# Two cross-attention query projections by Strassen's method in a fused decoder kernel

## The chip, the core and the metric

The kernel runs as one program on one core of a Trainium2 chip. The core has a matrix engine (TensorE, PE in the profile; its weight loads are PEld), VectorE (DVE), ScalarE (ACT), GpSimd (POOL) and SyncE (SP), which issues the DMAs. Each takes its own instructions in order, and they wait for each other by semaphores. The metric is the device time of one execution in microseconds: 1154.2 us is the median of three runs of the kernel before (1152.12 to 1158.6).

## What is computed

A decoder layer and a gated cross-attention layer, all in float32, over 16 sequences of 128 tokens and 512 features, with 16 heads of 32:

```python
ln_out = layernorm(hidden_states, ln1_s, ln1_b)
q, k, v = jnp.split(ln_out @ w_qkv + b_qkv, 3, axis=-1)
x = hidden_states + merge_heads(attention(q, k, v, ltor_mask)) @ w_ao + b_ao
ln_out = layernorm(x, ln2_s, ln2_b)
q = ln_out @ w_q + b_q                       # the product that is changed
k, v = jnp.split(encoder_states @ w_kv + b_kv, 2, axis=-1)
x = x + merge_heads(attention(q, k, v, cross_mask)) @ w_co + b_co
ln_out = layernorm(x, ln3_s, ln3_b)
x = x + gelu(ln_out @ w1 + b1) @ w2 + b2
# then: a gated cross-attention of x with the layer-normalized context, and its residual
```

The heads are split before each attention. Scores are scaled, masked, and turned into probabilities by a softmax.

## The kernel before

The 16 sequences are worked in four groups of four; a group's activations are 512 x 512 (512 features by 4 x 128 tokens), kept with features on the partitions in four chunks of 128. The decoder's attention is eight sections, one after the other: self-attention A0 to A3 (one a group), then cross-attention B0 to B3. An MLP and four gated sections D0 to D3 follow. A section is 16 steps, one for each unit of four heads (number 0 to 3) of a sequence.

`attend` (line 689) writes the order of all engines out by hand; nothing reorders it. In step k of a section TensorE does the scores of a new sequence (every fourth step), the mixing with the values of an earlier one (beside the scores) and its output projection `mo` (two steps after), and the products of the next section's `jobs`. VectorE turns a normalized unit (a 32 x 32 transpose; it is then sent to DRAM and fetched back as `pT`), takes reciprocals of the exponentials' sums, takes the least value of the unit masked in the step before, and scales new scores out of PSUM. ACT does the exponentials. POOL multiplies a unit by the reciprocals (`s<-s,sum`, called a normalization here), and adds the mask to a new unit (`s<-s,mask`). So POOL's mask of step k-1 releases VectorE's least values in step k, these release ACT's exponentials, and VectorE's reciprocal in step k+1 releases POOL's normalization there. `afterwards` (line 80) puts an operation off to the beginning of the next step, where `due` (line 83) issues what was put off, VectorE's first.

Beside section i, `jobs` computes query, key and value of section i+1, and `prepare(p)`, called in step p, prepares section i+2: layer normalization with statistics on VectorE, a power (`rstd`) and a row addition (`x<-x,bco_row`) on POOL, the way through DRAM that turns it (`back`), and in steps 12 to 15 the scaling into `lnT` by ACT. In steps 11 and 13 the first three sequences of x[g] are copied to DRAM, because their place in SBUF serves as scratch; `tokens_again` fetches them back in steps 5, 9 and 13 of the group's own section.

Key and value are computed by Strassen's method in Winograd's form (`block_product`, line 409): operands are cut into quarters of 256 x 256, sums of quarters are formed (`left_blocks` for a weight, `right_blocks` for activations, four additions each), and seven products of quarters, each four float32 matmuls of 128x256, are added up. Blocks 1, 6 and 7 share the PSUM bank mm0 and are copied out by ACT in the step that issues them; blocks 5 and 3 share the bank mm1; blocks 2 and 4 take one of two banks "pt" in turn with mixing and output projection. Blocks 2, 3, 4 and 5 are added into the result by VectorE, one step after. `CROSS_BLOCKS` (line 507) says which block is issued in which step: the key's in steps 4 to 11, the value's in steps 10 to 15. The query is computed directly, in four chunks of four matmuls of 128x512 (`project_chunk`, line 338) in steps 0, 1, 3 and 5, with the banks mm0 and mm1 in turn, and one copy by ACT each, put off by a step. The float32 matmuls stand twice in the profile's counts.

The key's and value's four token sums (`right_blocks(encT, tokens_at)`) are formed by POOL in steps 0 to 3, in scratch in x[g] and one in place. The weight sums of key and value are formed once, beside section A3: the key's by VectorE, the value's by POOL.

Of the kernel before, what the change touches and what calls it, by code (L numbers as in the profile page):

```python
# [54 lines left out]
def decoder_then_gated_cross_attention(ctx: ExitStack, tc: tile.TileContext, a: dict, out: bass.AP):  # L55
# [260 lines left out]
    def group_back(t, back, scale=None, bias=None, chunks=range(KC)):  # L316
        for k in chunks:
            chunk_back(t[:, k], back, k, scale, bias)
# [10 lines left out]
    def turn_squares(t, c):  # L329

        nc.vector.transpose(t[:, c], t[:, c])
# [32 lines left out]
    def halves(t):  # L364

        return [[t[:, 2 * i : 2 * i + 2, j * HF : (j + 1) * HF] for j in range(2)] for i in range(2)]
# [4 lines left out]
    def left_blocks(wt, t):  # L371


        (a11, a21), (a12, a22) = halves(wt)
        s3, s2, s4, s1 = (*t, a21)[:4]
        return [a11, a12, s4, a22, s1, s2, s3], [
            (s3, a11, a21, ALU.subtract), (s1, a21, a22, ALU.add), (s2, s1, a11, ALU.subtract),
            (s4, a12, s2, ALU.subtract),
        ]

    def right_blocks(actT, t):

        (b11, b12), (b21, b22) = halves(actT)
        t1, t2, t4 = t
        return [b11, b21, b22, t4, t1, t2, b12], [
            (t1, b12, b11, ALU.subtract), (t2, b22, t1, ALU.subtract), (b12, b22, b12, ALU.subtract),
            (t4, t2, b21, ALU.subtract),
        ]
# [20 lines left out]
    def block_product(out, left, right, turned, name, bias=None):  # L409

        product = quarter_matmuls(left, right, turned, name)
        (c11, c12), (c21, c22) = out

        def copy(dst, mm, half):

            if bias is None:
                nc.scalar.copy(dst, mm)
            else:  # L420
                for o in range(2):
                    nc.scalar.activation(dst[:, o], mm[:, o], AF.Identity, bias=col(bias[0], bias[1] + 2 * half + o))

        def add(dst, one, other, op=ALU.add):
            afterwards("dve", lambda: nc.vector.tensor_tensor(dst, one, other, op))

        mm5 = []

        def last_quarter():
            if len(mm5) == 2:  # L430
                add(c22, mm5[0], c21)

        def job(n):
            if n in (1, 6, 7):
                mm = product(n, "mm0", n == 1)
                copy({1: c11, 6: c12, 7: c21}[n], mm, int(n == 7))
                if n == 7:
                    mm5.append(None)
                    last_quarter()
            elif n == 5:  # L440
                mm5.insert(0, product(n, "mm1", True))
                last_quarter()
            elif n == 2:
                add(c11, product(n, "pt", True), c11)
            elif n == 4:
                add(c21, c21, product(n, "pt", True), ALU.subtract)
            elif n == 3:
                add(c12, product(n, "mm1", False), c12)

        return {n: lambda n=n: job(n) for n in range(1, 8)}  # L450
# [39 lines left out]
    def by_quarters(t):  # L490

        return [[t[:, 2 * j : 2 * j + 2, i * HF : (i + 1) * HF] for j in range(2)] for i in range(2)]
# [15 lines left out]
        {4: (1,), 7: (2, 6), 8: (5,), 9: (7, 4), 11: (3,)},  # L508
        {10: (1,), 11: (2,), 12: (6,), 13: (5, 7), 15: (4, 3)},
    )  # L510
    FIRST_CROSS_BLOCKS = {6: (1,), 7: (2, 6), 8: (5,), 9: (7, 4), 11: (3,)}, CROSS_BLOCKS[1]
    GATED_BLOCKS = (
# [10 lines left out]
    def blocks_plan(products, blocks):  # L523
        out = {}
        for jobs, steps_ in zip(products, blocks):
            for step, ns in steps_.items():
                out.setdefault(step, []).extend(jobs[n] for n in ns)
        return [(jobs, [step] * len(jobs)) for step, jobs in out.items()]
# [148 lines left out]
    def plan(*timed):  # L677

        out = {}
        for jobs, at_ in timed:  # L680
            for job, step in zip(jobs, at_, strict=True):
                out.setdefault(step, []).append(job)
        return out
# [321 lines left out]
    class CrossAttention(Section):  # L1005
# [6 lines left out]
        def prepare(self, p):  # L1012
            g, n = self.g, self.name
            if p == 0:
                if g == 0:
                    w["bco"] = load_row(a["L0_xattn_b_co"], "bco_row")
                self.ln, self.away = ln_tile(n), away_tile(n)
                self.encT = act_tile(f"e{g}", "enc")
            if p < 2 * GB:
                load_turned(self.encT, encoder_rows(g), p // 2, (2 * (p % 2), 2 * (p % 2) + 1))  # L1020
                q = p // 2
                if p % 2 == 0:
                    normalize_and_send(
                        x[g][:, q, :], self.ln[:, q], self.away, n, q, lambda: add_row(g, w["bco"], q)
                    )
            elif p == 9:
                self.back = receive(n, self.away)
                self.lnT = act_tile(n)
            elif p >= 12:
                group_back(self.lnT, self.back, "ln2_s", "ln2_b", [p - 12])  # L1030
            if p in (11, 13):

                for b in ((0, 1), (2,))[p == 13]:
                    keep_part(f"x_{n}", x[g], b)
            if p >= 2 * GB and p % 2 == 0:
                turn_squares(self.encT, p // 2 - GB)
            if g == 0 and p >= 3 * GB:
                load_cross("cq", p - 3 * GB)

        def jobs(self):  # L1040
            g, n, lnT, encT = self.g, self.name, self.lnT, self.encT
            mask = work.tile([P, 2, GB, S], F32, tag="mask", name=f"mask_{g}", bufs=2)
            self.ms, self.ma = mask[:, 0], mask[:, 1]
            nc.sync.dma_start(
                out=self.ms, in_=a["mask_Bx1xSxS2_ff1"][g * GB : (g + 1) * GB, 0].rearrange("b q k -> q b k")
            )
            qkv_tiles(self)
            tokens_at = [x[g][:, b].rearrange("p (o t) -> p o t", t=HF) for b in range(3)]
            token_sides, sums = right_blocks(encT, tokens_at)
            if g == 0:  # L1050
                self.begin()
            products = [
                block_product(halves(self.k), self.k_sides, token_sides, False, f"k_{n}", ("b_k", 0)),
                block_product(by_quarters(self.v), self.v_sides, token_sides, True, f"v_{n}"),
            ]
            return plan(
                ([lambda c=c: self.query_chunk(c) for c in range(KC)], [0, 1, 3, 5]),
                *blocks_plan(products, CROSS_BLOCKS if g else FIRST_CROSS_BLOCKS), ([lambda: mask_terms(self.ms, self.ma)], [7]),
                ([lambda o=o: nc.gpsimd.tensor_tensor(*o) for o in sums], [0, 1, 2, 3]),
                *(self.weights_begin() if g == 0 else decoder[NG + g - 1].tokens_again([5, 9, 13])),  # L1060
            )

# [1 line left out]
            project_chunk(self.q, w["cq"], self.lnT, c, f"q_{self.name}", "b_q", 0, ("mm0", "mm1")[c % 2])  # L1064

        v_bias = "b_cv", 0

        def tokens_again(self, at_, order=range(3)):
            return [([lambda b=b: fetch_part(f"x_{self.name}", x[self.g], b) for b in order], at_)]
# [391 lines left out]
    class FirstGated:  # L1461


        def prepare(self, p):
            if p == 0:
                self.raw = work.tile([P, GB, H], F32, tag="enc", name="enc_D0", bufs=2)
                self.ln, self.away = ln_tile("D0"), away_tile("D0")
            if p in (0, 1):
                for b in (2 * p, 2 * p + 1):
                    nc.sync.dma_start(out=self.raw[:, b, :], in_=a["ctx_2048"][b])  # L1470
            elif p >= 2 * GB:
                key, k = ("gk", "gv")[p // GB - 2], p % GB
                if k == 0:
                    w[key] = wpool.tile([P, KC, H], F32, tag="w", name=f"w_{key}")
                nc.sync.dma_start(out=w[key][:, k], in_=gated[key][:, k])
            if 2 <= p < 6:
                q = p - 2
                normalize_and_send(self.raw[:, q, :], self.ln[:, q], self.away, "D0", q)
            if p >= 12:
                if p == 12:  # L1480
                    next(in_mlp)
                ml.pieces.popleft()()
            if p in (9, 11):
                if p == 9:
                    self.back, self.part = receiver("a0", self.away)
                for m in range(2):
                    self.part(m + 2 * (p == 11))
            if p >= 12:
                if p == 12:
                    self.aT = act_tile("a0", "enc")  # L1490
                group_back(self.aT, self.back, "gamma", "beta", [p - 12])
# [339 lines left out]
```

## Time and profile before

| | before |
|---|---|
| median of three runs | 1154.2 us (1152.12 to 1158.6) |
| the profiled execution | 1150.03 us, its span 1148.3 us |
| granted TensorE clock in it | 1.0 |
| busy: PE, DVE, POOL, ACT | 1127.4, 743.3, 695.4, 611.3 us |
| section B0 (first scores to next section's) | 282.38 to 343.26 us |
| section B1 | 343.26 to 404.15 us |
| section B2 | 404.15 to 465.73 us |

A line of the order of time gives start and duration in us, engine, operation, what is written and read, shapes and count; group numbers are left out of names, so `mm_q_B` is the query of any cross-attention group. Where an engine was idle before, it says for how long and what ended that. Durations include the filling and emptying of an engine; back to back, instructions start closer together than their durations, and the distance of starts is what one costs. All instructions have the line of a helper, L51. `T_B` is lnT, `T_e` the encoder's activations, `s_B` a unit of scores, `sc_B` scores in PSUM. Spans on POOL are rough.

### The profile page before, as it was taken

How to read it: one execution, taken by the hardware profiler on the slowest of the kernel's cores; microseconds unless marked ns; L12 is line 12 of the kernel's file. 1: busy time of each engine (PE TensorE's matmuls, PEld its weight loads, DVE VectorE, ACT ScalarE, POOL GpSimd, SP SyncE). 2: the span in 40 equal slices, each digit the busy share in tenths (PEclk: the TensorE clock that was granted, in tenths of full speed). 3: DMA queues.
4: the chain of work that ended last, by engine and by line, in shares of the span. 5: the costliest groups of instructions: out<-in, count | busy, mean ns of one | idle time of the engine just before them, and what ended most of it. 6: DMA issues, size and time to landing. Idle time of an engine off the chain costs nothing. (4 is left out here: it accounts for less than half of the span.)

```text
span 1148.3 us, 22191 instructions
## 1 busy us (share of the span) xinstructions
PE 1127.4 (98%) x7246; PEld 870.1 (76%) x7246; DVE 743.3 (65%) x1919; ACT 611.3 (53%) x2142; POOL 695.4 (61%) x633
## 2 busy tenths in 40 slices
PE   8999999999999999999999999999999999999998
PEld 7877777667575757546788888888888877878885
DVE  6678988888877776987664634443342237767764
ACT  3467676767676776774231333233222337777663
POOL 6798888788868685773333414443343168545874
PEclk9999999999999999999999999999999999999999
DMA  6588878999888879999786596697446827988975
GB/s 222 153 216 233 221 217 221 260 231 264 211 229 217 229 213 255 294 284 296 243 259 232 183 285 188 198 280 266 156 147 220 268 70 191 246 245 233 266 223 182
DMA packets 325284, 259.81 MB, mean 226 GB/s; under 512 B 83560, under 2 KB 280624, under 8 KB 320304
## 3 DMA queue, kind: packets, MB, share of 16 engines
q1 hardware_dynamic: 325128, 258.38, 78.4%
q8 instruction: 58, 0.95, 0.4%
q14 instruction: 58, 0.48, 0.1%
q10 hardware_dynamic: 40, 0.01, 0.0%
HBM read 163.94 MB, written 94.37 MB: 225 GB/s over the span
## 5 line engine op out<-in xcount | busy, mean ns | idle before, releaser
L51 DVE TENSOR_TENSOR h<-h,h 128x512 f32<-128x512 f32 x80 | 54.8, 686 | 114.4 <-PE h L51 114.3
L51 ACT ACTIVATE h<-h 128x512 f32<-128x512 f32 x64 | 40.3, 630 | 160.9 <-DVE h L51 160.9
L51 ACT ACTIVATE s_A<-s_A,mn_A 128x128 f32<-128x128 f32 x256 | 99.4, 391 | 46.8 <-issue 24.1
L51 ACT ACTIVATE s_B<-s_B,mn_B 128x128 f32<-128x128 f32 x256 | 99.4, 392 | 31.1 <-issue 18.2
L51 POOL TENSOR_TENSOR s_D<-s_D,sum_D 128x512 f32<-128x512 f32 x64 | 66.8, 1043 | 56.1 <-DVE sum_D L51 53.7
L51 ACT ACTIVATE s_D<-s_D,mn_D 128x128 f32<-128x128 f32 x256 | 99.1, 392 | 0.4 <-issue 0.4
L51 POOL TENSOR_TENSOR s_B<-s_B,sum_B 128x512 f32<-128x512 f32 x64 | 67.2, 1051 | 51.5 <-DVE sum_B L51 33.5
L51 POOL TENSOR_TENSOR s_A<-s_A,sum_A 128x512 f32<-128x512 f32 x64 | 66.9, 1046 | 30.4 <-DVE sum_A L51 24.5
L51 POOL TENSOR_TENSOR s_A<-s_A,ma 128x512 f32<-128x512 f32 x64 | 82.3, 1286 | 5.1 <-DVE s_A L51 4.1
L51 POOL TENSOR_TENSOR s_B<-s_B,mask 128x512 f32<-128x512 f32 x60 | 76.8, 1280 | 2.2 <-DVE s_B L51 1.3
L51 POOL TENSOR_TENSOR rstd_aD<-rstd_aD,mhalf 128x1 f32<-128x1 f32 x12 | 6.6, 550 | 115.0 <-DVE rstd_aD L51 101.5
L51 POOL TENSOR_TENSOR sh<-h 128x512 f32<-128x512 f32 x32 | 40.8, 1274 | 50.5 <-ACT h L51 49.6
L51 PE MATMUL h<-T_C,w 128*128 128x256 f32 x256 | 61.2, 382 | 2.2 <-DVE h L51 2.2
L51 PE MATMUL h<-T_C,t 128*128 128x256 f32 x256 | 60.6, 379 | 1.0 <-DVE h L51 1.0
L51 PE MATMUL h<-sx,t 128*128 128x256 f32 x256 | 60.7, 380 | 0.5 <-POOL sx L51 0.5
L51 PE MATMUL o<-t,sh 128*128 128x256 f32 x256 | 60.5, 379 | 0.0
L51 PE MATMUL o<-w,h 128*128 128x256 f32 x256 | 60.5, 379 | 0.0
L51 PE MATMUL o<-t,h 128*128 128x256 f32 x256 | 60.5, 379 | 0.0
L51 DVE CUSTOM_DVE_ANT_0 s_D<-sc_D,gmask 128x128 f32<-128x128 f32 x256 | 57.2, 283 | 1.3 <-DMA turned_x<-x_D 0.7
L51 PE MATMUL mo_B<-w_co,mT_B 128*128 128x512 f32 x128 | 57.5, 592 | 0.0
L51 PE MATMUL mo_A<-w_ao,mT_A 128*128 128x512 f32 x128 | 57.5, 592 | 0.0
L51 PE MATMUL mm_q_B<-T_B,w_cq 128*128 128x512 f32 x128 | 57.4, 596 | 0.0
(335 smaller groups left out, 2998.1 us busy)
## 6 DMA issues: line engine op xcount, KB each, us to landing
t<-kept SPq DMA_DIRECT2D x24, 1024.0 KB, 8.2
away_A<-s_A SPq DMA_DIRECT2D x64, 256.0 KB, 3.1
pT_A<-away_A SPq DMA_DIRECT2D x128, 128.0 KB, 3.3
away_B<-s_B SPq DMA_DIRECT2D x64, 256.0 KB, 4.1
pT_B<-away_B SPq DMA_DIRECT2D x128, 128.0 KB, 3.3
away_D<-s_D SPq DMA_DIRECT2D x60, 256.0 KB, 3.6
pT_D<-away_D SPq DMA_DIRECT2D x120, 128.0 KB, 2.8
w<-in_L_xattn_w_dram SPq DMA_DIRECT2D x24, 512.0 KB, 5.9
```

The source lines that it names most:

```text
L51: return lambda *args, **kw: self.tc.keep_in_program_order(call(*args, **kw))
```

## The change

Groups 2 and 3 (the third and fourth) compute the cross-attention's query by `block_product` too; groups 0 and 1 stay as they were. The steps of its blocks are in `QUERY_BLOCKS`. The four sums of the query weight are formed once by VectorE in steps 11 to 14 of section B0, in the buffer that will later hold the weight "gk", and one of them in place in the query weight. The four sums of a group's query tokens are formed by POOL, one in step 15 of the section before and three in steps 0, 1 and 3; their scratch is the preceding group's x, whose three sequences have been put away in DRAM and not yet been fetched back. For these two groups the key's and value's token sums move from steps 0, 1, 2, 3 to step 13 of the section before and steps 2, 4, 5. The later load of "gk" finds its buffer allocated already. The query's PSUM use changes from mm0 and mm1 in turn to mm0, mm1 and two turns of "pt".

```diff
+    QUERY_BLOCKS = {0: (1,), 1: (2, 6), 3: (5, 7), 5: (4, 3)},
...
             elif p >= 12:
                 group_back(self.lnT, self.back, "ln2_s", "ln2_b", [p - 12])
+            if p == 15 and self.by_blocks:
+                self.query_sides, self.query_sums = right_blocks(self.lnT, decoder[NG + g - 1].tokens_at())
+                nc.gpsimd.tensor_tensor(*self.query_sums.pop(0))
...
+            if p == 13 and self.by_blocks:
+                self.begin_tokens()
+                nc.gpsimd.tensor_tensor(*self.sums.pop(0))
...
-            tokens_at = [x[g][:, b].rearrange("p (o t) -> p o t", t=HF) for b in range(3)]
-            token_sides, sums = right_blocks(encT, tokens_at)
             if g == 0:
                 self.begin()
+            if not self.by_blocks:
+                self.begin_tokens()
...
+            by_pool = lambda sums: [lambda o=o: nc.gpsimd.tensor_tensor(*o) for o in sums]
+            if self.by_blocks:
+                query = block_product(
+                    halves(self.q), CrossAttention.q_sides, self.query_sides, False, f"q_{n}", ("b_q", 0)
+                )
+                queries = (
+                    *blocks_plan([query], QUERY_BLOCKS), (by_pool(self.query_sums), [0, 1, 3]),
+                    (by_pool(self.sums), [2, 4, 5]),
+                )
+            else:
+                queries = (
+                    ([lambda c=c: self.query_chunk(c) for c in range(KC)], [0, 1, 3, 5]), (by_pool(self.sums), [0, 1, 2, 3]),
+                )
+                if g == 1:
+                    queries += (self.query_weights(),)
             return plan(
-                ([lambda c=c: self.query_chunk(c) for c in range(KC)], [0, 1, 3, 5]),
+                *queries,
                 *blocks_plan(products, CROSS_BLOCKS if g else FIRST_CROSS_BLOCKS), ([lambda: mask_terms(self.ms, self.ma)], [7]),
-                ([lambda o=o: nc.gpsimd.tensor_tensor(*o) for o in sums], [0, 1, 2, 3]),
...
+        by_blocks = property(lambda self: self.g > 1)
+
+        def tokens_at(self):
+            return [x[self.g][:, b].rearrange("p (o t) -> p o t", t=HF) for b in range(3)]
+
+        def begin_tokens(self):
+            self.token_sides, self.sums = right_blocks(self.encT, self.tokens_at())
+
+        def query_weights(self):
+
+            todo = []
+
+            def add(n):
+                if n == 0:
+                    w["gk"] = wpool.tile([P, KC, H], F32, tag="w", name="w_gk")
+                    at_ = [w["gk"][:, m].rearrange("p (o t) -> p o t", t=HF) for m in range(3)]
+                    CrossAttention.q_sides, sums = left_blocks(w["cq"], at_)
+                    todo.extend(sums)
+                nc.vector.tensor_tensor(*todo[n])
+
+            return [lambda n=n: add(n) for n in range(4)], [11, 12, 13, 14]
...
-                if k == 0:
+                if k == 0 and key not in w:
                     w[key] = wpool.tile([P, KC, H], F32, tag="w", name=f"w_{key}")
```

More of the change, by code (lines that the diff above doesn't have):

```diff
@@ L1047, in jobs @@
             qkv_tiles(self)
-            tokens_at = [x[g][:, b].rearrange("p (o t) -> p o t", t=HF) for b in range(3)]
-            token_sides, sums = right_blocks(encT, tokens_at)
             if g == 0:
                 self.begin()
+            if not self.by_blocks:
+                self.begin_tokens()
             products = [
-                block_product(halves(self.k), self.k_sides, token_sides, False, f"k_{n}", ("b_k", 0)),
-                block_product(by_quarters(self.v), self.v_sides, token_sides, True, f"v_{n}"),
-            ]
+                block_product(halves(self.k), self.k_sides, self.token_sides, False, f"k_{n}", ("b_k", 0)),
+                block_product(by_quarters(self.v), self.v_sides, self.token_sides, True, f"v_{n}"),
+            ]
+            by_pool = lambda sums: [lambda o=o: nc.gpsimd.tensor_tensor(*o) for o in sums]
[13 more added lines that the diff above has]
+                    queries += (self.query_weights(),)
             return plan(
-                ([lambda c=c: self.query_chunk(c) for c in range(KC)], [0, 1, 3, 5]),
+                *queries,
                 *blocks_plan(products, CROSS_BLOCKS if g else FIRST_CROSS_BLOCKS), ([lambda: mask_terms(self.ms, self.ma)], [7]),
-                ([lambda o=o: nc.gpsimd.tensor_tensor(*o) for o in sums], [0, 1, 2, 3]),
                 *(self.weights_begin() if g == 0 else decoder[NG + g - 1].tokens_again([5, 9, 13])),
```

## The prediction

> **What bounds the kernel now.** I read the page's busy times first, then TensorE's waits, then TensorE's order of time in the sections that the change touches, then the queues of the engines that feed it.
>
> ```profile
> PE 1127.4 (98%) x7246; PEld 870.1 (76%) x7246; DVE 743.3 (65%) x1919; ACT 611.3 (53%) x2142; POOL 695.4 (61%) x633
> ```
>
> TensorE is busy for 1127.4 of 1148.3 us. Its waits over the whole trace sum to about 19 us, and the only one between 282 and 466 us (sections B0 to B2) is 0.6 us. So a matmul that goes is worth its time, unless another engine now becomes late. TensorE in section B1, the query of the third group beside the attention of the second:
>
> ```profile
> 344.37 7.13 PE L51 MATMUL mm_q_B<-T_B,w_cq 128*128 128x512 f32 x16
> 351.34 3.60 PE L51 MATMUL mo_B<-w_co,mT_B 128*128 128x512 f32 x8
> 354.77 3.60 PE L51 MATMUL mm_q_B<-T_B,w_cq 128*128 128x512 f32 x8
> ...
> 362.24 3.60 PE L51 MATMUL mm_q_B<-T_B,w_cq 128*128 128x512 f32 x8
> 365.67 3.60 PE L51 MATMUL mo_B<-w_co,mT_B 128*128 128x512 f32 x8
> 369.11 1.89 PE L51 MATMUL mm_k_B<-T_e,w_ck 128*128 128x256 f32 x8
> 370.83 1.89 PE L51 MATMUL mm_k_B<-x,sums_c 128*128 128x256 f32 x8
> ```
>
> Starts, not durations, give the price: a query chunk takes 3.43 us (362.24 to 365.67), a block of four matmuls of 256 columns 1.72 us (369.11 to 370.83). Nothing is idle between them. The engines beside it, by quarters of a section (span, then busy us of PE, PEld, DVE, ACT, POOL):
>
> ```profile
> 343.26:359.31 16.05, 16.05 (x101) 7.80 (x97) 13.04 (x32) 11.29 (x43) 16.05 (x16) 1.00 0.88 216
> 359.31:373.67 14.36, 14.36 (x109) 9.31 (x105) 11.03 (x24) 9.73 (x37) 11.28 (x12) 1.00 0.84 204
> ...
> 404.15:420.19 16.04, 16.04 (x100) 7.79 (x96) 11.49 (x27) 9.33 (x40) 14.74 (x15) 1.00 0.78 218
> ```
>
> In the first quarter of B1 POOL is busy for 16.05 of 16.05 us, as long as TensorE. In B2 it has 1.3 us left. That is where the change adds POOL work and takes TensorE time.
>
> **TensorE.** A query is now 4 chunks: 13.9 us (6.97, 3.53 and 3.43 by the starts, with 0.1 us at each change of shape). Seven blocks take 7 x 1.725 and two changes of shape, 12.3 us. Gain 1.65 us a group, 3.3 us for two. The one wait in the range, 0.62 us at 421.99 (key block 1 of B2's step 4, for the ACT copy of a query chunk out of the bank mm0), should go too: the chunk's copy was put off by a step, the block's copy is issued in its own step. Nothing else is late there: block 7 of step 3 would end at about 417.4, ACT copies it in 0.84 us, and key block 1 comes at about 419.5. Most that can be gained: 3.9 us.
>
> **ACT.** Four copies of 128x512 (0.68 us) become six of 128x256 (0.42): 2.7 to 2.5 us a group. Nothing.
>
> **VectorE.** Four additions out of PSUM a group at 0.60 us spacing (2.4 us), and once, in B0's steps 11 to 14, four weight sums. The same sums for the key's weight stand in the trace, beside POOL:
>
> ```profile
> 233.52 3.97 DVE L51 TENSOR_TENSOR sums_c<-w_ck 128x512 f32<-128x512 f32 x1
> 237.53 0.69 DVE L51 TENSOR_TENSOR w_ck<-w_ck 128x512 f32<-128x512 f32 x1
> ...
> 241.12 0.68 DVE L51 TENSOR_TENSOR sums_c<-w_ck 128x512 f32<-128x512 f32 x1
> 241.83 1.64 DVE L51 TENSOR_TENSOR sums_c<-w_ck,sums_c 128x512 f32<-128x512 f32 x1
> ```
>
> ```profile
> 233.42 1.07 POOL L51 TENSOR_TENSOR s_A<-s_A,sum_A 128x512 f32<-128x512 f32 x1
> 234.42 1.30 POOL L51 TENSOR_TENSOR s_A<-s_A,ma 128x512 f32<-128x512 f32 x1
> 235.64 1.30 POOL L51 TENSOR_TENSOR x<-x,bco_row 128x512 f32<-128x512 f32 x1
> ```
>
> The sum that took 3.97 us ends only after POOL's run of three, 233.42 to 236.94; free of POOL it is 0.68. The price of four is between 2.7 us and, if two stand behind such a run, 9.3. In steps 11 and 12 of B0 they fall into VectorE's idle time (0.92 us at 327.1, 3.01 us at 331.9). The third starts about 332.1, when POOL has a mask addition and the new key sum of step 13 before it, to 334.7; so the reciprocal that started at 334.88 starts about 336.0. From 334.88 to 345.8 VectorE has no gap, so the fourth (0.62 and some 0.2 behind POOL) stays too. I take 1.9 us of lateness at the end of B0; ends 0.6 (no POOL in the way) and 7.9 (both at 3.97). I take the low part since here POOL's next normalization waits for VectorE's own reciprocal, which ends its run.
>
> The Trainium skill ("SBUF — State Buffer", section "Who interferes with whom") says that a VectorE instruction with both inputs in SBUF and a GpSimd one that reads SBUF exclude each other for the whole instruction. The 3.97 us row agrees and is longer than one instruction. By the rule with one POOL instruction of 1.28 us each, the last two sums would leave VectorE 3.2 us late in place of 1.9, and the total would be an estimated 1155.4; without any exclusion it would be 0.6 late, and the total 1152.8.
>
> **POOL.** Spacings in the full stretch: sum or row addition 1.23, normalization 1.00, mask 1.23, rstd 0.51. Eight query sums are added (two groups); the key's four are moved from steps 0 to 3 to the step 13 before and 2, 4, 5. Step 13 has 2.7 us idle, so the first key sum is hidden there, and the copy of x that it must wait for is issued at 325.8 and lands in 4.0 to 6.5 us, by 332.3. The query sum in step 15 finds 0.24 us idle at 341.1 and delays the rest by 1.0. Steps 0 to 3 keep four sums; steps 4 and 5 get two more.
>
> *Section B1.* Before, POOL ends step 4 at 363.65. After: 363.65 + 1.0 + 1.9 + 1.23 (key sum in step 4) = 367.8. VectorE is in order: least values of that unit (0.57), two score scalings (1.20), a transpose (0.62), then the eviction of query block 4 (0.60) end at 370.8. Key block 2 in step 7 needs that bank, one of the two "pt". TensorE would be there at 369.11 - 1.65 = 367.5, so it waits 3.3 us. Then step 5 on POOL ends at 371.3, VectorE's additions, statistics, transpose, least values and scaling take it to 374.3 and the output addition to 374.9; TensorE has two blocks to 374.35 and waits 0.55 for the bank of av. Sum 3.85 us against a gain of 1.65: **2.2 us lost in B1.** The transfers of probabilities are not in it: issued three steps ahead of their use (10 us), they land in 3.3.
>
> *Section B2.* There are no row additions on POOL and no weight sums before. POOL starts step 0 at 404.48 + 1.0; steps 0 and 1 are 3.46 us each, 2 to 4 3.97 each; step 4 ends at 424.3 (before: 423.8). Eviction of block 4 at 424.3 + 0.57 + 1.20 + 1.22 = 427.3; TensorE is at key block 2 at 430.69 - 1.65 - 0.62 = 428.4. No wait, with 1.1 us to spare: **2.27 us gained.**
>
> *Other queues.* No DMA is added. SP's fetches of x (steps 5, 9, 13) wait for other readers, the query's blocks of steps 1, 3 and 5 and POOL's sum of step 3, all done by then or within the step; behind a late one the fetches of pT would queue, which have 5 us. The tile for the weight sums takes the place in the ring that it had later. The self-attention's output weight, whose buffer it overwrites, was last read at 324.4, and VectorE's sum stands behind the addition that waits for the same matmuls.
>
> **Sum.** -2.27 + 2.2 = -0.1 us on the profiled execution's 1150.0 us (span 1148.3). Its time is 4.2 us under the median of the three runs, 1154.2, which is what I forecast against: **1154 us**. The runs themselves span 6.5 us; 0.5% (5.8 us) is about what a measurement of this kernel can tell from no change.
>
> **Rivals.** *The gain whole*: POOL's lateness never reaches TensorE. For it: key and value blocks run without a gap beside the same helpers. Against: POOL's full first quarter. 1154.2 - 3.9 = 1150.3. *B2 is late too*: 1.1 us is a thin margin, and three sums (3.7 us) more on POOL could eat it; if it loses its gain and 0.3 more, 1154.2 + 2.2 + 0.3 = 1156.7. *Slower*: the last weight sums of B0 stand behind POOL for 3.97 us each. VectorE is then 7.9 us late, 6.0 more than taken, and all of it reaches TensorE: 1154.2 - 0.1 + 6.0 = 1160.1. It decides from 7.8 us of lateness on; for it the 3.97 row, against it that POOL waits for VectorE there. That seven blocks cost no less than four chunks is ruled out by the starts above.
>
> **How the numbers follow.** My case 0.52 (its own range 1151 to 1157, the runs' scatter), whole gain 0.20, B2 late 0.20, slower 0.08. No case is faster by 5.8 us; scatter around the whole gain gives 0.05. Slower by over 0.5% gets the rival's 0.08 and 0.03 of scatter. Same 0.84. The range goes from 1150.3 less 2 of scatter, 1148.5, to the slower rival, 1159.5.
>
> **What would show it.** Right: query blocks at 1.72 us in B1 and B2; TensorE waiting in B1 near steps 7 and 8 for VectorE's query or x addition, 3 to 4 us; none in B2; POOL without a gap from B1's step 15 to 6; w_gk sums on VectorE at over 1 us. Wrong: no TensorE wait in B1 (then 2 to 4 us faster), or waits for DMA or in other sections, of which this argument knows nothing.

## The result and the profile after

The changed kernel takes 1155.51 us (median of 22 runs, 1153.3 to 1161.22) against 1153.18 us for the kernel before (22 runs): a ratio of 1.0023, 95% interval 1.0012 to 1.0033. It is slower by 2.3 us by the two medians and by 2.65 us by the ratio, about a quarter of a per cent, where the forecast had 0.1 us of gain and 1154 us. (A ratio here is formed over the runs of both kernels and is not the quotient of the two medians.) The forecast's 1154 us was set against 1154.2 us, the median of three runs of the kernel before; over 22 runs that kernel takes 1.0 us less. The time lies within the range, and the loss within the 0.5% that was called the same; but over 22 runs the loss can be told from zero, and the forecast's sum had the other sign. The profiled execution has a span of 1151.5 us (before: 1148.3).

The busy times of the page, after:

```profile
PE 1125.9 (98%) x7294; PEld 879.4 (76%) x7294; DVE 751.1 (65%) x1931; ACT 610.5 (53%) x2146; POOL 704.7 (61%) x641
```

TensorE has less to do than before (1125.9 against 1127.4 us) in a longer span, so what was lost is waiting. TensorE in section B1 in order of time (start, us, engine, line, operation, shapes, count; in brackets the idle time before it and what ended it):

```profile
343.95 3.72 PE L51 MATMUL mm_q_B<-T_B,w_cq 128*128 128x256 f32 x16
347.51 1.89 PE L51 MATMUL mm_q_B<-x,w_gk 128*128 128x256 f32 x8
349.24 3.60 PE L51 MATMUL mo_B<-w_co,mT_B 128*128 128x512 f32 x8
352.67 1.89 PE L51 MATMUL mm_q_B<-x,w_cq 128*128 128x256 f32 x8
354.40 1.89 PE L51 MATMUL mm_q_B<-T_B,w_gk 128*128 128x256 f32 x8
...
360.16 1.89 PE L51 MATMUL mm_q_B<-x,w_cq 128*128 128x256 f32 x8
361.89 1.89 PE L51 MATMUL mm_q_B<-T_B,w_gk 128*128 128x256 f32 x8
363.62 3.60 PE L51 MATMUL mo_B<-w_co,mT_B 128*128 128x512 f32 x8
369.35 1.99 PE L51 MATMUL mm_k_B<-T_e,w_ck 128*128 128x256 f32 x8 [2.13 <-DVE q_B L51]
371.18 1.89 PE L51 MATMUL mm_k_B<-x,sums_c 128*128 128x256 f32 x8
373.39 1.28 PE L51 MATMUL av_B<-pT_B,v_B 128*32 128x128 f32 x32 [0.33 <-DVE x L51]
...
381.52 1.99 PE L51 MATMUL mm_v_B<-w_cv,T_e 128*128 128x256 f32 x8 [0.36 <-ACT k_B L51]
```

The seven query blocks take 1.73 us each by their starts. The output projection at 363.62 comes 20.77 us after the section's first scores (342.85); before it came 22.41 us after them (343.26 to 365.67). That is 1.64 us gained. Then TensorE waits three times, 2.13, 0.33 and 0.36 us.

VectorE in the same place, which releases the first of these waits:

```profile
366.22 0.69 DVE L51 TENSOR_REDUCE mn_B<-s_B 128x4 f32<-128x512 f32 x1 [0.45 <-POOL s_B L51]
366.82 1.28 DVE L51 TENSOR_TENSOR s_B<-sc_B,mask 128x512 f32<-128x512 f32 x2
368.02 0.70 DVE L51 STREAM_TRANSPOSE ln_B<-ln_B 128x512 f32<-128x512 f32 x1
368.64 0.65 DVE L51 TENSOR_TENSOR q_B<-q_B,mm_q_B 128x512 f32<-128x512 f32 x1
```

POOL's mask of that unit, before and after:

```profile
362.42 1.30 POOL L51 TENSOR_TENSOR s_B<-s_B,mask 128x512 f32<-128x512 f32 x1
```

```profile
364.91 1.27 POOL L51 TENSOR_TENSOR s_B<-s_B,mask 128x512 f32<-128x512 f32 x1
```

The least values wait for this mask. By POOL's spacing of 1.23 us it is done at 366.14 (before: 363.65), 2.9 us later than before when both are counted from the section's first scores. The eviction of query block 4, which stands behind two scalings and a transpose, ends at 369.3. The same three stretches as before by engine (span, then busy us of PE, PEld, DVE, ACT, POOL, then clock, DMA share, GB/s):

```profile
342.85:357.23 14.38, 14.38 (x116) 10.83 (x113) 11.73 (x27) 10.44 (x42) 14.38 (x14) 1.00 0.83 208
357.23:374.61 17.38, 14.92 (x117) 10.91 (x113) 13.95 (x30) 9.99 (x42) 16.45 (x16) 1.00 0.75 192
405.72:420.10 14.38, 14.38 (x116) 10.83 (x113) 11.47 (x26) 9.36 (x38) 14.38 (x15) 1.00 0.80 228
```

POOL is now busy without a gap in the first quarter of B1 and of B2 both, and for 16.45 of 17.38 us in B1's second quarter. The weight sums on VectorE in B0, where the forecast feared POOL most:

```profile
324.72 0.68 DVE L51 TENSOR_TENSOR w_gk<-w_cq 128x512 f32<-128x512 f32 x1
...
328.18 0.89 DVE L51 TENSOR_TENSOR w_cq<-w_cq 128x512 f32<-128x512 f32 x1
...
331.43 0.68 DVE L51 TENSOR_TENSOR w_gk<-w_cq 128x512 f32<-128x512 f32 x1
...
336.93 0.79 DVE L51 TENSOR_TENSOR w_gk<-w_cq,w_gk 128x512 f32<-128x512 f32 x1
```

None takes more than 0.89 us. POOL's masks next to the last three of them:

```profile
327.23 1.29 POOL L51 TENSOR_TENSOR s_B<-s_B,mask 128x512 f32<-128x512 f32 x1
...
331.59 1.65 POOL L51 TENSOR_TENSOR s_B<-s_B,mask 128x512 f32<-128x512 f32 x1
...
335.90 1.27 POOL L51 TENSOR_TENSOR s_B<-s_B,mask 128x512 f32<-128x512 f32 x1
```

The sections, from first scores to the next section's first scores, and B3 from its first scores to its last, in us:

| | B0 | B1 | B2 | B3, to its last scores |
|---|---|---|---|---|
| before | 60.88 | 60.89 | 61.58 | 39.72 |
| after | 60.89 | 62.87 | 60.51 | 40.69 |

B1 loses 1.98 us, B2 gains only 1.07, and B3, in which the change alters nothing, loses 0.97. Together 1.88 us of the 2.65 us that the ratio gives. The rest of the difference of the two profiled spans (3.2 us) lies mostly in waits for transfers of probabilities later in the program (in D0, for example, 1.06 us at 972.86). Those of the gated sections add up to between 1.2 and 3.8 us in the profiles of the kernels told of here, with no order in them, so I do not put them down to the change.

B2's missing gain shows on ACT, in step 12. First before, then after (scaling of the first quarter of the gated attention's context, `T_a`):

```profile
455.79 0.81 ACT L51 ACTIVATE T_a<-back_a,vcols 128x512 f32<-128x512 f32 x1 [0.72 <-DMA back_a<-turned_D]
```

```profile
457.59 0.81 ACT L51 ACTIVATE T_a<-back_a,vcols 128x512 f32<-128x512 f32 x1 [3.29 <-DMA back_a<-turned_D]
```

Beside B2 the first group of the gated attention is prepared: the context's tokens go to DRAM and are fetched back turned (`back_a`), in two halves, issued by SP in steps 9 and 11; ACT scales them from step 12 on. ACT reaches that instruction at 454.30, 48.6 us into the section, where before it was there 50.9 us into it (455.07): TensorE's and the helpers' gain, 2.3 us, is there. But the data are not. Four exponentials stand behind it on ACT, VectorE's reciprocal behind these, and behind that an eviction that TensorE needs. VectorE after, and TensorE:

```profile
459.97 0.18 DVE L51 RECIPROCAL sum_B<-sum_B 128x4 f32<-128x4 f32 x1 [6.89 <-ACT s_B L51]
460.07 0.66 DVE L51 TENSOR_REDUCE mn_B<-s_B 128x4 f32<-128x512 f32 x1
460.64 1.28 DVE L51 TENSOR_TENSOR s_B<-sc_B,mask 128x512 f32<-128x512 f32 x2
461.83 0.68 DVE L51 TENSOR_TENSOR v_B<-mm_v_B,v_B 128x512 f32<-128x512 f32 x1
```

```profile
462.57 1.99 PE L51 MATMUL mm_v_B<-sums_c,T_e 128*128 128x256 f32 x8 [0.28 <-DVE v_B L51]
465.01 1.28 PE L51 MATMUL av_B<-pT_B,v_B 128*32 128x128 f32 x32 [0.45 <-DVE x L51]
...
500.37 3.70 PE L51 MATMUL mo_B<-w_co,mT_B 128*128 128x512 f32 x8 [0.55 <-ACT mT_B L51]
```

Before, none of these three matmuls waited. B3 also has a wait for probabilities in front of its last scores, in every kernel told of here and between 0.28 and 2.83 us; without it B3 takes 38.23 us before and 39.18 after (1.49 and 1.51 us taken off).

### The profile page after: what moved, and what is told of

Its sections match the earlier page's. It is cut to its first block, busy times and chain, and to the rows that moved or that the text cites. A ratio compares the mean times of both kernels' runs of the same rounds, so it can differ in the third digit from the quotient of the medians.

```text
span 1151.5 us, 22311 instructions
## 1 busy us (share of the span) xinstructions
PE 1125.9 (98%) x7294; PEld 879.4 (76%) x7294; DVE 751.1 (65%) x1931; ACT 610.5 (53%) x2146; POOL 704.7 (61%) x641
## 4 chain that ended last, share of the span: by engine, by line
PE 58%; POOL 7%; DVE 5%; issue 4%; DMA 4%; ACT 1%; SPq 1%; POOLq 0%; DVEq 0%; ACTq 0%
PE o L51 16%; PE h L51 15%; PE mm_v_D L51 3%; PE mm_q_D L51 3%; PE mm_k_D L51 3%; PE mm_v_B L51 3%; PE mo_B L51 2%; PE mm_q_B L51 2%; PE mm_k_B L51 2%; POOL x L51 2%; SPq L51 1%; POOL s_B L51 1%; PE mo_A L51 1%; POOL s_D L51 1%; PE av_D L51 1%
## 5 line engine op out<-in xcount | busy, mean ns | idle before, releaser
L51 PEld LDWEIGHTS h<-T_C,w 128*128 128x128 f32 x256 | 48.1, 190 | 10.5 <-DVE h L51 3.9
```

The source lines that it names most:

```text
L51: return lambda *args, **kw: self.tc.keep_in_program_order(call(*args, **kw))
```

## The experiments

Theory 1: B1 loses because POOL is late and VectorE and a PSUM bank pass it on; B2 (with B3) does not get its gain because the turned transfer of the gated group arrives at its own time. Rivals: the weight sums of B0 carry B1's lateness; the fourth group's blocks cost what they save by themselves (POOL late in B2 too); what the blocks take from TensorE they give back in copies and evictions wherever they are. Ratios are against runs of the kernel before on the same chip, with 95% intervals. Lengths of sections are from one profiled execution of each kernel; B1 comes out the same to 0.03 us (62.84 to 62.87) in the three kernels whose B1 is that of the changed kernel and ran at full clock.

**One group alone.** The fourth, whose weight sums then stand in B1, and then the third, where the edit also gives one weight sum a place of its own, since the fourth group still reads the whole weight:

```diff
-                if g == 1:
+                if g == 2:
                     queries += (self.query_weights(),)
...
-        by_blocks = property(lambda self: self.g > 1)
+        by_blocks = property(lambda self: self.g > 2)
```

```diff
-        by_blocks = property(lambda self: self.g > 1)
+        by_blocks = property(lambda self: self.g == 2)
```

> Only the fourth group's query by blocks; its weight sums move to steps 11 to 14 of section B1. Theory 1 (the third group's query costs 2.0 us in B1, because POOL and VectorE are late there, and the fourth's gain in B2 is given back because ACT waits in B2's step 12 for the transfer back_a): B1 as long as before (60.9 us) or up to 0.7 longer for the weight sums, B2 and B3 together within 0.5 us of before, total 0 to +1 us against before. Rival (the fourth group's gain in B2 is real and only B1 loses): total -1 to -2.3 us against before.

> Only the third group's query by blocks (one weight sum gets a place of its own, as the fourth group still needs the whole weight). Theory 1: B1 about 62.9 us against 60.9, TensorE waiting there for VectorE's query addition by about 2 us, B2 as before; total +1.5 to +2.5 us against before, most of the whole change's loss. Rival (the loss is spread over later sections and is not B1's own): B1 longer by less than 1 us, total under +1 us.

The fourth alone: 1152.98 against 1153.09 us, 1.0001 (0.9990 to 1.0012). B1 is 60.88, as before, B2 60.95, B3 38.64 without its waits for probabilities (0.61 and 2.83 us, more than in any other run). The third alone: 1154.47, 1.0009 (0.9994 to 1.0023), less than the 1.5 to 2.5 us expected but with them in its interval; B1 is 62.84, B2 61.58, with this wait in B1:

```profile
368.51 1.99 PE L51 MATMUL mm_k_B<-T_e,w_ck 128*128 128x256 f32 x8 [2.11 <-DVE q_B L51]
```

So B1's loss belongs to the third group by itself. Of the fourth group's 2.3 us, B2 keeps 0.63 and B3 gives back 0.41, and the time does not move; in its trace ACT waits 3.48 us at `T_a`, though nothing was late in B1. (There and in the run without row additions the profile names a fetch of `pT_B` as what ended that wait; the instruction itself reads `back_a`.) With the third group alone ACT waits there 1.56 us; TensorE does not wait in B2's last steps, and 0.21 us in B3 for ACT, where the changed kernel waits 0.55. B3 without its wait for probabilities is 38.72 us in that run, 0.49 more than before, although B2 got no shorter there. So some of this transfer's lateness comes without any gain in B2, and no run here shows from what.

**The turned transfer earlier.** All four parts of `back_a` in step 9, in the changed kernel and in the kernel before:

```diff
-            if p in (9, 11):
-                if p == 9:
-                    self.back, self.part = receiver("a0", self.away)
-                for m in range(2):
-                    self.part(m + 2 * (p == 11))
+            if p == 9:
+                self.back, self.part = receiver("a0", self.away)
+                for m in range(4):
+                    self.part(m)
```

> The changed kernel, but all four parts of the transfer back_a are issued in step 9 of B2, where two of them were issued in step 11. Theory 1: ACT no longer waits for back_a in B2's step 12 (3.3 us in the changed kernel), B2 is 59.3 to 59.5 us long (60.5 in the changed kernel), B3 no longer loses 1 us; total -2 us against the changed kernel, about +0.5 against before. Rival (the last steps of B2 are late for another reason, such as the queue of pT transfers or VectorE): the wait of ACT goes but B2 and B3 together get less than 0.7 us shorter, total +2 us or more against before.

> The kernel before with the same transfer issued in step 9. ACT waited 0.7 us for it before, and TensorE did not wait in B2's last steps, so both theories expect the time of before within 0.7 us. If it gains 2 us as in the changed kernel, the transfer bounds the section without the change too and the comparison tells nothing of the change.

The changed kernel: 1151.64 us, 0.9987 (0.9975 to 0.9999), 1.5 us less than before where I expected about 0.5 more. B2 is 59.24, 2.34 less than before, and ACT finds its data:

```profile
454.73 0.81 ACT L51 ACTIVATE T_a<-back_a,vcols 128x512 f32<-128x512 f32 x1
```

The kernel before: 1152.19, 0.9990 (0.9973 to 1.0008), B2 unchanged at 61.58. The 0.72 us that ACT waited there cost nothing, since TensorE did not need it earlier. With the transfer moved, the fourth group's blocks are worth their full 2.3 us in B2, B3 is 38.23 us without its wait for probabilities (0.28), and the changed kernel goes from 1.0023 to 0.9987. By the two ratios that is about 4 us, more than the 2.2 us found in B2 and B3; where the rest lies isn't shown. Without the blocks the move does nothing in B2. B1 is 63.29 us in this run, 0.42 more than in the changed kernel with the same work: behind its wait of 2.15 us key block 2 ran at a granted clock of 0.52 (3.46 us by the starts, 1.83 in the changed kernel at 1.00), and the two later waits are gone. Why the clock fell here and not there isn't shown.

**What makes the transfer late.** The gated key weight `gk` is loaded in steps 8 to 11 of B2 in four pieces of 256 KB on the same queue. Three of them left out (the gated attention's key of the first group is then formed from other numbers):

```diff
-                nc.sync.dma_start(out=w[key][:, k], in_=gated[key][:, k])
+                if key != "gk" or k == 3:
+                    nc.sync.dma_start(out=w[key][:, k], in_=gated[key][:, k])
```

> The changed kernel without three of the four 256 KB loads of the weight gk in steps 8 to 10 of B2 (the gated layer's first key is then computed from wrong numbers there). Theory (the transfer back_a is late because the DMA engines are full and the queue before it holds these loads): ACT's wait for back_a in step 12 falls from 3.3 us to under 1, B2 is 59.2 to 60.0 us (60.5 in the changed kernel). Rival (it is late only because it is issued in step 11, behind VectorE's and POOL's work on SP's queue): the wait stays above 2.5 us.

1151.33 against 1151.35 us, 0.9999 (0.9989 to 1.0009), from 1.0023. B1 stays at 62.85, B2 is 59.24 and B3 38.23 without its wait of 1.30 us for probabilities: 2.34 us gained in B2 and nothing given back. ACT in this run:

```profile
453.95 0.81 ACT L51 ACTIVATE T_a<-back_a,vcols 128x512 f32<-128x512 f32 x1 [0.39 <-DMA back_a<-turned_D]
```

SP's queue before the change, after it, and in this run:

```profile
443.90 3.73 SPq L51 DMA_DIRECT2D pT_B<-away_B  x4
448.40 0.34 SPq L51 DMA_DIRECT2D w_gk<-kept_gk  x1
448.82 1.17 SPq L51 DMA_DIRECT2D back_a<-turned_D  x2
```

```profile
444.30 3.79 SPq L51 DMA_DIRECT2D pT_B<-away_B  x4
449.30 0.34 SPq L51 DMA_DIRECT2D w_gk<-kept_gk  x1
449.68 0.91 SPq L51 DMA_DIRECT2D back_a<-turned_D  x2
```

```profile
443.18 1.93 SPq L51 DMA_DIRECT2D pT_B<-away_B  x4
445.23 0.34 SPq L51 DMA_DIRECT2D w_gk<-kept_gk  x1
446.05 0.93 SPq L51 DMA_DIRECT2D back_a<-turned_D  x2
```

From the second issue to ACT's start are 7.9 us in both (457.59 - 449.68, 453.95 - 446.05). What differs between these two is when SP issues it: 3.6 us earlier in this run, of which the section's own start explains 0.74 (404.98 for 405.72). SP works in order. The four fetches of `pT_B` in front take 1.93 us to issue in place of 3.79, and SP then stands still for 0.1 us in place of 1.2. So it is the load of `gk` on the queue, more than TensorE's progress, that sets when the turned data come. The kernel before had the same load, and its fetches took as long to issue (3.73 us): counted from the section's first scores the second half was issued at 44.7 us there and at 44.0 after the change, but it was 7.0 us from issue to ACT's start there and 7.9 after (8.7 in the next run). How the load lengthens SP's issues isn't shown by this run; the DMA engines' busy share from 440 to 457 us is about 1 in both (1.00 and 1.06).

**POOL in B1.** The row additions of the fourth group's preparation (`x<-x,bco_row`, four POOL instructions of 1.28 us, which start between 352.27 and 377.79 after the change) left out, so that this group's output bias is missing:

```diff
-                        x[g][:, q, :], self.ln[:, q], self.away, n, q, lambda: add_row(g, w["bco"], q)
+                        x[g][:, q, :], self.ln[:, q], self.away, n, q,
+                        None if g == 3 else lambda: add_row(g, w["bco"], q),
```

> The changed kernel without the four row additions of POOL in B1 (the cross-attention's output bias is left out for the fourth group; 3.7 us of POOL's work in steps 2 to 6 is away, and 1.2 in step 8). Theory (POOL's queue is what makes VectorE late in B1): TensorE's wait of 2.1 us for VectorE's query addition goes, B1 is 59.3 to 59.9 us (62.9 in the changed kernel, 60.9 before). Rival (VectorE's own four additions and the weight sums, 2.4 and 2.5 us, are what is too much): the wait stays above 1 us and B1 above 61.5.

1152.28 against 1153.46 us, 1.0001 (0.9984 to 1.0018). The wait of 2.13 us is gone and B1 is 60.43: 2.44 us less than after the change and 0.46 less than before it. I expected 59.3 to 59.9; the mixing's wait (0.28) and the value block's (0.36) with their restarts stay. Less POOL work takes away the wait on VectorE's query eviction, which is what theory 1 says. And B2, which starts 2.6 us earlier now, is 1.8 us longer, 62.31:

```profile
459.19 0.18 DVE L51 RECIPROCAL sum_B<-sum_B 128x4 f32<-128x4 f32 x1 [8.70 <-ACT s_B L51]
```

```profile
461.79 1.99 PE L51 MATMUL mm_v_B<-sums_c,T_e 128*128 128x256 f32 x8 [2.08 <-DVE v_B L51]
```

ACT's first `T_a` starts at 456.81, after 5.10 us of waiting. ACT was ready for it 3.4 us earlier than in the kernel before (451.71 against 455.07), but SP issued the transfer's second half only 0.66 us earlier (448.16 against 448.82). What B1 got back was lost again at the same transfer.

**The weight sums.** In place of three of them SP loads part of the query weight into the buffer, so that the queries of the third and fourth group are formed from other numbers; VectorE has no sum to do:

```diff
-                nc.vector.tensor_tensor(*todo[n])
+                if n < 3:
+                    nc.sync.dma_start(
+                        out=w["gk"][:, n].rearrange("p (o t) -> p o t", t=HF),
+                        in_=a["L0_xattn_w_q"][0:HALF, 0:HF].rearrange("(k p) n -> p k n", p=P),
+                    )
```

> The changed kernel without VectorE's four weight sums in B0 (their places are filled by three DMA loads of quarters of the weight, so the third and fourth groups' queries are not the right ones). Theory: the sums made VectorE 0.7 us late at the end of B0, so TensorE's wait of 2.1 us in B1 shrinks to about 1.5 and B1 to 62.0 to 62.5 us; most of B1's loss stays. Rival (the weight sums are most of it): B1 under 61.3 us.

B1 is 62.14 us, 0.73 less than after the change, and the wait before key block 2 is 1.40 in place of 2.13. So the sums carry 0.7 us of B1's loss of 2 us, and the larger part is POOL's. The whole program does not show it: 1.0030 (1.0012 to 1.0048), with a profiled span of 1150.0.

**Both put right.** The row additions of the fourth group taken out as above and put into steps 9 to 12, where POOL has idle time, and the early transfer; with the blocks, and then without them on the kernel before:

```diff
+            if g == 3 and 9 <= p <= 12:
+                add_row(g, w["bco"], p - 9)
```

> The changed kernel with the fourth group's row additions in steps 9 to 12 of B1, where POOL has idle time, and the transfer back_a issued in step 9 of B2. Theory: B1 59.3 to 60.0 us, B2 59.2 to 59.5, both of the lost gains come back: -3 to -4.5 us against before. Rival (the later sections take what is gained, or steps 9 to 12 become late in place of 2 to 6): -1.5 us or less.

> The kernel before with the same two moves and no blocks for the query. Theory: B1 stays at 60.9 us, since TensorE had no wait there, B2 at 61.6, only the transfer's 1 us in B3 is gained: -0.3 to -1.5 us against before. What is then left between this and the same moves in the changed kernel, 2.5 to 3.5 us, is the worth of the two queries by blocks. Rival (the moves are worth as much without the blocks): both alike within 1 us.

With the blocks 1148.17 against 1153.46 us, 0.9969 (0.9956 to 0.9983): B1 60.39, B2 59.24. Without them 1151.57, 0.9995 (0.9984 to 1.0007). The same two moves are worth nothing that can be measured in the kernel before, and turn the blocks from a loss of 0.23% into a gain of 0.31%; between the two ratios, each with an interval of about 0.13% to either side, the blocks are worth about 0.26%, 3.0 us, of the 3.9 us that the forecast gave as the most.

**The last wait in B1.** After this ACT's copy of key block 7 still comes 0.35 us late for the value block that takes the same bank, and two VectorE instructions of `mask_terms` stand in step 7 in front of what ACT's exponentials wait for. They are moved to step 13 in B1, beside the edits above:

```diff
-                *blocks_plan(products, CROSS_BLOCKS if g else FIRST_CROSS_BLOCKS), ([lambda: mask_terms(self.ms, self.ma)], [7]),
+                *blocks_plan(products, CROSS_BLOCKS if g else FIRST_CROSS_BLOCKS), ([lambda: mask_terms(self.ms, self.ma)], [13 if g == 2 else 7]),
```

> The changed kernel with late row additions and the early transfer, and VectorE's two mask terms (1.4 us) in step 13 of B1 in place of step 7. Theory (what is left of B1's waits, 0.25 us for the output addition and 0.35 for ACT's copy with 0.6 us of restarts, is VectorE's lateness in steps 7 and 8): B1 59.3 to 59.9 us (60.4 with the two moves alone), total -3.5 to -4.7 us against before. Rival (POOL or ACT hold B1 there, not VectorE's own work): B1 stays at 60.2 or more.

B1 is 59.75, 0.64 less, and one wait is left in it:

```profile
370.87 1.28 PE L51 MATMUL av_B<-pT_B,v_B 128*32 128x128 f32 x32 [0.24 <-DVE x L51]
```

1146.76 against 1151.35 us, 0.9966 (0.9953 to 0.9979). By the interval it is the kernel above, and both beat the kernel before and the changed kernel.

## Why the prediction was wrong

- **TensorE's price: right.** 1.64 us gained a group, 1.65 forecast. The wait of 0.62 us in B2 went too: B2 was 2.34 us shorter wherever nothing else held it up, 2.27 forecast.
- **B1: right in mechanism and nearly in size.** 1.98 us lost, 2.2 forecast; POOL, VectorE, the bank "pt", key block 2, in that order. Terms inside were off and cancelled; that the two numbers lie so close is luck. The weight sums made VectorE 0.7 us late at the end of B0, not 1.9, so POOL ended step 4 at 366.14, not 367.8 (0.4 of that is the earlier start of the whole section), and the wait was 2.13, not 3.3; the mixing's wait was 0.33, not 0.55. And I missed a wait, 0.36 us for ACT's copy of key block 7, and that TensorE comes back from each wait slower (the mixing's start to the scores 1.22 us behind a wait, 1.02 without one).
- **The rule on exclusion.** By the rule that I took from the Trainium skill ("SBUF — State Buffer", section "Who interferes with whom") the sums would have cost more than my 1.9 us. The runs go the other way: 0.68 to 0.89 us each. That speaks against how I used the rule, with a whole POOL instruction in front of each of the last two sums, and not against the rule itself. In each pair that overlapped, the one that started second got longer: VectorE's sums at 328.18 and 336.93, by 0.2 and 0.1 us, which started up to 0.3 us before POOL's mask was done; and POOL's mask at 331.59, 1.65 us in place of 1.28, which started 0.16 us after a sum. The 3.97 us row of section A3, where the sum started 0.1 us into a run of three and ended 0.55 us after it, was a poor guide to this place.
- **B2: wrong, and this is the step that failed.** "No wait, with 1.1 us to spare: 2.27 us gained" was right as far as it looked, for POOL was full there and no query or key block waited. But it looked only at the first half of the section, where the change puts its work. The transfer `back_a` in steps 9 to 12 was not in the reckoning: after "No DMA is added" only the fetches of x and of pT were looked at. A transfer needs no new load beside it to become late: here it became late when the rest came sooner (in the fourth group's run alone ACT's wait grew from 0.72 to 3.48 us). The trace of before said so, in ACT's 0.72 us of waiting at 455.79. A section shortened by 2.27 us from its front would make that about 3 us (0.72 + 2.27; 3.29 measured, the sum of an issue 0.7 us earlier in the section and 0.9 us more from issue to ACT's start), and behind it stand ACT's exponentials, VectorE's reciprocal and the eviction that TensorE needs. That cost 1.27 us in B2 (2.34 - 1.07) and 0.95 in B3, of which up to 0.49 may be the lateness that the third group's run shows without a shorter B2. With these 2.2 us the forecast's sum would have been +2.1 us, against 1.88 in the sections and 2.7 by the ratio of the runs.
- **The rivals.** "B2 is late too" came nearest: 2.5 us lost against the kernel before, and 2.65 measured by the ratio; but not by its mechanism, POOL's margin. "The gain whole" is what the program becomes once both waits are out (0.9969 against 1150.3/1154.2 = 0.9966). The slower rival, from the weight sums, did not come.
- **Its signs.** "Wrong: ... waits for DMA or in other sections, of which this argument knows nothing" is what the trace showed, with ACT's wait for a transfer and the loss in B3. Of the signs of being right, query blocks at 1.72 us came, POOL's full stretch came, and the wait near step 7 came, 2.13 us (2.8 with the two behind it) in place of 3 to 4; weight sums of over 1 us and a B2 without waits did not come. The ends of the range do not quite follow from their own sums (1150.3 less 2 is 1148.3, and the slower rival was 1160.1), and nothing rests on that.

What stays open: the 0.8 us of the ratio's 2.65 that these sections don't account for, what made the transfer later with the third group alone, and what sets the waits for probabilities at B3's end and in the gated sections.

## What to carry to other kernels

When work on the bounding engine gets shorter, a transfer that is held up by its own queue need not come sooner. List every transfer in the section that gets shorter, to its end, with the wait that it already causes on any engine, however small and wherever: that wait plus the gain is a first estimate of the new wait (here 3.0 for 3.29 and 3.48 us; it also grew by 0.8 us without a gain), and what stands behind it in order is what will be late. And when a change adds to a helper engine that is full in that section, look for work on it that isn't urgent: four row additions moved to idle steps took 2.5 us out of B1 here (62.87 in the changed kernel, 60.39 with the two moves, of which the other is in B2).

## What was not expected of the hardware

- Issuing a DMA had no fixed price on SP: four fetches of 128 KB took 1.93 us to issue with `gk` left out and 3.79 with it, at the same place. As SP works in order, the load of `gk` so made `back_a`, which does not need it, 2.9 us late (3.6 less the 0.74 of the section's start).
- The two-input sums on VectorE cost 0.68 to 0.89 us here and 3.97 us beside POOL's run of three in A3. The lengthened instruction can also be POOL's (1.65 against 1.28 us): in each of these pairs it was the one that started second.
